# Level-1 sums of a two-level Strassen product made in PSUM instead of on VectorE

## The chip, the core and the metric

The kernel runs on one core of a Trainium2 chip. Its time is the device time of one execution in microseconds (us); less is better. The engines are TensorE (PE; its weight loads are shown as PEld), VectorE (DVE), ScalarE (ACT), GpSimd (POOL) and SyncE (SP). PE adds its products up in PSUM, eight banks of 128 partitions x 512 fp32 columns; DVE and ACT read and write PSUM and SBUF. DMAs are issued from SP and from ACT: an issue from ACT stands in ACT's queue among its other work.

## What is computed

Two graph layers over N = 3327 nodes with D = 512 features, in fp32, with a dense 3327 x 3327 matrix `adj`:

```python
# layer 0: attention with adj added twice to the scores
h = relu(layernorm(x));  q, k, v = h @ Wq.T + bq, h @ Wk.T + bk, h @ Wv.T + bv
x = x + softmax(q @ k.T / sqrt(D) + adj + adj, axis=-1) @ v
# layer 1: normalised convolution with A2 = adj + I
h = relu(layernorm(x));  temp = A2 @ h @ W.T
d = diagonal(A2) ** -0.5
x = x + relu((d[:, None] * A2 * d[None, :]) @ temp)
```

Up to about 620 us the kernel makes the scores and their exponentials. From there on it makes three large products of the same shape, called g = 0, 1, 2: the exponentials by h, A2 by h, and A2 by `temp` (scaled). The change lies in these three.

## The kernel before

**Two levels of Strassen (Winograd's form).** Each of the three products is split into 2 x 2 blocks and made from seven block products, in the order `ORDER` = p5, p1, p6, p7, p2, p3, p4 (level 1). Each of them is made for two strips s = 0, 1 of the output (quarter widths `Q` = 448 and 384 columns), again from seven products (level 2). The output stands transposed in SBUF as four regions per strip, r11, r12, r21, r22, in the buffers `cts`.

**Steps.** A (g, r, s) has seven steps: t = 0 to 5, which take the 26 row tiles in pairs, and t = None for the thirteenth row of tiles, without Strassen. A step t = 0 to 5 multiplies seven times (L918, L919; each product stands as two MATMUL records in the trace), into seven banks named p1 to p7 by level 2. At t=0 the order is p6, p7, p5, p2, p3, p4, p1, at t = 1 to 5 p1 is first. p1, p6, p7 and p5 end with t=5. The step t=None multiplies four times (L911), into p2, p3, p4 and p8, and p8 takes the bank that p1 had.

**Gathering.** At the end of t=5 `Gather.first` (L942) has ACT copy p1 to SBUF (L947) and DVE make three sums and differences with p6, p7, p5 (L948 to L951). At the end of t=None `rest` adds p2, p3, p4 and p8 to the four quarters (L964 to L967); L964 is the one that frees bank p2, L966 the one that frees p4. For p5 and p1 the result lands in a region at once (`place`). For the other five it lands in a spare buffer `to`, and `settle` (L969) does the level-1 sums on DVE, in instructions of 896 or 768 columns: for p6 r12 = to − r11 (L973), for p7 r21 = to + r12 (L975) and two more (L976, L977), for p2, p3 and p4 one addition to r11, r12 or r21 (L980). The very last product (g=2, p4, s=1) adds its banks straight into the region.

**The order of the work.** `run(k)` (L1230) writes out step k, and `in_order` (L1295) keeps each engine's instructions, ACT's and SP's too, in the order of the program. In a step: the DMA for the step three later; the loads named in `between` (those from ACT are L1018 in `attend_load` and L1088 in `finish_load`); the matmuls; the delayed stores `deliver` (L797, L93, from ACT); for t=None `rest`; then what is left for DVE: the sums of the left operands for the step two later (`four_sums`, L175 to L177, with L901 for the diagonal), `settle`, and the remaining tasks in `between` (right operands, L882 to L886 and L182 to L185; `Job`, L1002; `attend`, L1020; `attended`, L1028; `finish`, L1118).

**Work beside it.** In g = 0, from p3 strip 1 to the end, every step finishes one row of attention: `attend` multiplies by the value weights on PE (L1011) and normalises on DVE and POOL; one step later, t=None included, `attended` has DVE make `nb` (L206), ACT make the activation (L1030), and ACT issue its store (L1031). In g = 1, from p3 strip 1 to the start of g = 2, `Temp` multiplies by the weights of layer 1 (L1072, L1076, L1078). In g = 2 `finish` transposes and stores the rows of the result.

Of the kernel before, what the change touches and what calls it, by code (L numbers as in the profile page):

```python
# [29 lines left out]
ORDER = ("p5", "p1", "p6", "p7", "p2", "p3", "p4")  # L30
# [6 lines left out]
PAIRS = 6  # L37
# [3 lines left out]
Q = tuple(n * P // 2 for n in HT)  # L41
# [6 lines left out]
def graph_layers_kernel(  # L48
# [29 lines left out]
    nc = tc.nc  # L78
# [31 lines left out]
    def bank(k, name):  # L110
        return banks.tile([P, BW], F32, name=name, tag=f"bank{k}")
# [323 lines left out]
    ps = [bank(k, "mm") for k in range(DC)]  # L435
    begun = h_transposed(TURN[0], psum_ring(6, 7, 4, 5))
    weighed = half(12, [P, D], "weighed")
    for c in range(DC):
# [8 lines left out]
        for r in range(DC):  # L447
            nc.tensor.matmul(ps[r], w_q[c // 2][:, c % 2, r * P : (r + 1) * P], w_k[c // 2][:, c % 2],
                             start=c == 0, stop=c == DC - 1)
# [165 lines left out]
    steps = [(n, t) for n in range(len(groups)) for t in range(HALF)]  # L615
# [32 lines left out]
    with in_order(*(e.engine for e in (nc.vector, nc.tensor, nc.gpsimd, nc.sync))):  # L648
# [9 lines left out]
        k = len(steps)  # L658
# [28 lines left out]
    ROLE = {"p1": 0, "p6": 2, "p7": 4, "p5": 6, "p2": 7, "p3": 1, "p4": 5, "p8": 3}  # L687

    def seven():
        return {r: bank(ROLE[r], r) for r in ("p6", "p7", "p5", "p2", "p3", "p4", "p1")}  # L690
# [199 lines left out]
    class Step:  # L890


        def __init__(self, g, r, s, t, right):
            self.g, self.r, self.s, self.t, self.right = g, r, s, t, right

        def load(self):
            self.a, self.diagonals = left(self.g, self.s, A_OF[self.r], self.t)
# [9 lines left out]
        def multiply(self, ps):  # L907
            a, b, w = self.a, self.right.b, Q[self.s]
            if self.t is None:
                for k, (y, z) in enumerate(((0, 0), (0, 1), (1, 0), (1, 1))):  # L910
                    yield nc.tensor.matmul(ps[("p2", "p3", "p4", "p8")[k]][:, :w], b[:, z], a[:, 0, y],  # L911
                                           start=k == 3, stop=True)
                return
            o, first = self.o, [("p1", 0, a[:, 0, 0])]
            seven = [("p6", 5, o[:, 2]), ("p7", 6, o[:, 0]), ("p5", 4, o[:, 1]),
                     ("p2", 2, a[:, 1, 0]), ("p3", 3, o[:, 3]), ("p4", 7, a[:, 1, 1])]

            for r, i, m in seven + first if self.t == 0 else first + seven:  # L918
                yield nc.tensor.matmul(ps[r][:, :w], b[:, i], m, start=self.t == 0,  # L919
                                       stop=self.t == PAIRS - 1 and r in ("p1", "p5", "p6", "p7"))  # L920

    flags = []

    class Gather:


        def __init__(self, r, s, last):
            ct, hw, qw = cts[s], H[s], Q[s]

            def region(y, z):  # L930
                return [ct[y][2 * z + k] for k in range(2)]

            self.r, self.last, self.place = r, last, {"p5": (1, 1), "p1": (0, 0)}.get(r)
            self.to = region(*self.place) if self.place else [cts["to"][k][:, :hw] for k in range(2)]
            self.width = qw
            self.spots = ((0, slice(0, qw)), (1, slice(0, qw)), (0, slice(qw, hw)), (1, slice(qw, hw)))
            self.regions = [region(y, z) for y in range(2) for z in range(2)]

        def parts(self, of):

            return [of[k][:, w] for k, w in self.spots]

        def first(self, ps):

# [11 lines left out]
        def rest(self, ps, names=("p2", "p3", "p4", "p8")):  # L956
            p = {k: ps[k][:, : self.width] for k in ("p2", "p3", "p4", "p8")}
            if self.last:
                for o, k in zip(self.parts(self.regions[2]), p):
                    if k in names:  # L960
                        nc.vector.tensor_add(o, o, p[k])
                return
            c11, c12, c21, c22 = self.parts(self.to)
            nc.vector.tensor_add(c11, c11, p["p2"])  # L964
            nc.vector.tensor_sub(c12, p["p3"], c12)
            nc.vector.tensor_add(c21, c21, p["p4"])  # L966
            nc.vector.tensor_add(c22, c22, p["p8"])  # L967

        def settle(self):  # L969
            r11, r12, r21, r22 = self.regions  # L970
            for k, to in enumerate(self.to):
                if self.r == "p6":
                    yield nc.vector.tensor_sub(r12[k], to, r11[k])  # L973
                elif self.r == "p7":
                    yield nc.vector.tensor_add(r21[k], to, r12[k])  # L975
                    yield nc.vector.tensor_sub(r12[k], r22[k], r12[k])  # L976
                    yield nc.vector.tensor_sub(r22[k], r21[k], r22[k])  # L977
                elif not self.place and not self.last:
                    t = {"p2": r11, "p3": r12, "p4": r21}[self.r]
                    yield nc.vector.tensor_add(t[k], t[k], to)  # L980

    def where(i):

# [138 lines left out]
    every = (*range(PAIRS), None)  # L1122
    rights = {(g, r, t): Right(g, r, t) for g in range(3) for r in ORDER for t in every}
    steps = [Step(g, r, s, t, rights[g, r, t]) for g in range(3) for r in ORDER for s in range(2) for t in every]
# [3 lines left out]
    def number_of(g, r, s, t):  # L1128
        return ((g * len(ORDER) + r) * 2 + s) * len(every) + t
# [5 lines left out]
    for g in range(3):  # L1135
        for n, r in enumerate(ORDER):
            for t, e in enumerate(every):
                k = number_of(g, n, 0, t)
# [9 lines left out]
    for n, job in enumerate(jobs):  # L1148
        k = k0 + n * (k1 - k0) // len(jobs)
# [15 lines left out]
    k = number_of(0, 5, 1, 2)  # L1165
# [6 lines left out]
    k = number_of(1, 5, 1, 2)  # L1172
    for n in range(0, NT, 2):
        if steps[k].t is None:
            k += 1
        w = Temp(*ROW[n : n + 2])
# [5 lines left out]
    for (n, s, t), its in {  # L1182
# [4 lines left out]
        for i, when in zip(its, (between, within)):  # L1187
            if i is not None:
                k = number_of(2, n, s, t)
# [8 lines left out]
    k = number_of(1, 4, 0, 0)  # L1198
# [13 lines left out]
    banks_of, gathers = {}, {}  # L1212
    resting = []
# [6 lines left out]
    def first_of(parts):  # L1220
        while parts:
            for _ in parts[0]:
                yield
            parts.pop(0)

    def do(part, n=None):
        for _ in itertools.islice(part, n):
            pass

    def run(k):  # L1230
        step, now[0] = steps[k], k
        if k + 3 < len(steps):
            steps[k + 3].load()
        if step.t == 0:
            banks_of.update(seven())
        if not cts:
            set_up()
        if step.t is None:
            banks_of["p8"] = bank(ROLE["p1"], "p8")
        t = step.t  # L1240
        for what, args in between.get(k, ()):
            if "load" in what.__name__:
                what(*args)
        if t == PAIRS - 1:
            gathers[step.r, step.s] = Gather(step.r, step.s, k == len(steps) - 2)
        gatherer = gathers.get((step.r, step.s))
        weighs = any((k, j) in inserted for j in range(7))
        if k in sums_of and not waiting:
            do(sums_of.pop(k)())
        for j, _ in enumerate(itertools.chain((None,), step.multiply(banks_of))):  # L1250
            for w, n in inserted.get((k, j), ()):
                w.product(n)
            if j == 4 and t == PAIRS - 1 and gatherer.last:
                gatherer.first(banks_of)
            for what, args in within.get(k, ()) if j == 4 else ():
                what(*args)
            if j == 2 and k in sums_of:

                sums = sums_of.pop(k)()
                do(sums, 4)  # L1260
                waiting.insert(1, sums)
            elif weighs and j > 0:
                do(first_of(waiting), 2)
        deliver(k)
        if t is None:
            do(first_of(waiting))
            if gatherer.last:
                flags.append(nc.values_load(bad, min_val=0, max_val=1))
                for n, names in enumerate((("p2", "p3"), ("p4", "p8"))):
                    gatherer.rest(banks_of, names)  # L1270
                    for i in range(20 + 3 * n, 23 + 3 * n):
                        turn_last(i)
            else:
                gatherer.rest(banks_of)
        added = 2 + (t is None)
        waiting.append(steps[k + 2].sums() if k + 2 < len(steps) else iter(()))
        if t == PAIRS - 1 and not gatherer.last:
            do(first_of(waiting))
            gatherer.first(banks_of)
        if t is None and gatherer.r == "p7":  # L1280
            settle = gatherer.settle()
            resting.extend((itertools.islice(settle, 3), settle))
            added -= 1
        elif t is None:
            waiting.append(gatherer.settle())
        elif resting:
            waiting.append(resting.pop(0))
            added += 1
        waiting.append(flow([(what, args) for what, args in between.get(k, ()) if "load" not in what.__name__]))
        if (k + 1, 0) not in inserted and (k + 1, 1) not in inserted:  # L1290
            do(first_of(waiting))
        while len(waiting) > added:
            do(waiting.pop(0))
# [386 lines left out]
```

## Time and profile before

| | us |
|---|---|
| median of 3 runs (2164.09 to 2168.61) | 2165.39 |
| the profiled execution's own time | 2165.84 |
| its span, first to last instruction | 2164.1 |
| PE, matmuls | 2148.5 (99%) |
| DVE | 1675.6 (77%) |
| ACT | 237.0 (11%) |

The mean granted clock of PE is 0.999 of full speed. Matmuls of level 2 follow each other every 0.376 us (448 columns) or 0.323 us (384), two to a product. In the profile's lists a name such as L964 is a line of the kernel; "ACTq" is a DMA issue on ACT; a row of a timeline has start and length in us, engine, line, operation, output<-input, shapes, and in brackets the idle time of that engine before it and what ended it. Names like `part` and `ct` are buffers that share their place with others, and `p` stands for all banks p1 to p8.

### The profile page before, as it was taken

How to read it: one execution, taken by the hardware profiler on the slowest of the kernel's cores; microseconds unless marked ns; L12 is line 12 of the kernel's file. 1: busy time of each engine (PE TensorE's matmuls, PEld its weight loads, DVE VectorE, ACT ScalarE, POOL GpSimd, SP SyncE). 2: the span in 40 equal slices, each digit the busy share in tenths (PEclk: the TensorE clock that was granted, in tenths of full speed). 3: DMA queues.
4: the chain of work that ended last, by engine and by line, in shares of the span. 5: the costliest groups of instructions: out<-in, count | busy, mean ns of one | idle time of the engine just before them, and what ended most of it. 6: DMA issues, size and time to landing. Idle time of an engine off the chain costs nothing.

```text
span 2164.1 us, 20995 instructions
## 1 busy us (share of the span) xinstructions
PE 2148.5 (99%) x6364; PEld 1189.9 (55%) x6364; DVE 1675.6 (77%) x3270; ACT 237.0 (11%) x363; POOL 51.5 (2%) x62
## 2 busy tenths in 40 slices
PE   9999999999999999999999999999999999999998
PEld 5555555555555555555454555555666655555555
DVE  7479888888887688877778778886676667778686
ACT  5312211112110000000101000000011100000011
POOL 2000000000000000000111000000000000000000
PEclk9999999999999999999999999999999999999999
DMA  8678898888988899889797889886646468766695
GB/s 302 211 257 302 296 311 278 306 293 301 328 306 301 292 370 329 280 289 314 263 311 259 304 289 368 308 302 221 208 133 217 137 193 286 246 194 210 217 304 197
DMA packets 298670, 586.01 MB, mean 271 GB/s; under 512 B 31274, under 2 KB 166324, under 8 KB 298548
## 3 DMA queue, kind: packets, MB, share of 16 engines
q1 hardware_dynamic: 263254, 515.10, 70.8%
q10 hardware_dynamic: 35294, 69.48, 8.8%
q8 instruction: 53, 0.87, 0.2%
q14 instruction: 69, 0.57, 0.1%
HBM read 416.63 MB, written 167.84 MB: 270 GB/s over the span
## 4 chain that ended last, share of the span: by engine, by line
PE 93%; DVE 5%; DMA 1%; issue 1%; POOL 0%; SPq 0%; ACT 0%; DVEq 0%
PE p L919 55%; PE Y L553 13%; PE Z L553 6%; PE p L911 5%; PE p L1011 4%; PE pw L1072 3%; PE X L553 3%; PE Y L409 2%; PE Z L409 1%; PE pt L1101 1%; DVE part L175 0%; DMA rows<-row 0%; PE X L409 0%; DVE st L196 0%; DMA xt<-in_x_dram 0%
## 5 line engine op out<-in xcount | busy, mean ns | idle before, releaser
L919 PE MATMUL p<-part,b 128*128 128x448 f32 (+1 forms) x3528 | 1261.6, 513 | 0.4 <-DVE part L176 0.2
L919 PEld LDWEIGHTS p<-part,b 128*128 128x128 f32 x3528 | 668.0, 190 | 534.4 <-issue 283.5
L553 PE MATMUL Y<-qt,hp 128*128 128x448 f32 (+1 forms) x832 | 308.2, 513 | 2.1 <-DVE g L557 1.7
L175 DVE TENSOR_TENSOR part<-part 128x896 f32<-128x896 f32 (+1 forms) x252 | 256.8, 1019 | 57.0 <-DMA part<-p 24.6
L553 PEld LDWEIGHTS Y<-qt,hp 128*128 128x128 f32 x832 | 157.8, 190 | 135.9 <-issue 72.7
L553 PE MATMUL Z<-qt,hp 128*128 128x384 f32 (+1 forms) x416 | 162.3, 512 | 0.0
L177 DVE TENSOR_TENSOR part<-part,part 128x448 f32<-128x448 f32 (+1 forms) x219 | 129.4, 591 | 15.3 <-PE p L919 0.5
L176 DVE TENSOR_TENSOR part<-part,part 128x448 f32<-128x448 f32 (+1 forms) x219 | 129.4, 591 | 7.2
L911 PE MATMUL p<-part,b 128*128 128x448 f32 (+1 forms) x336 | 124.2, 513 | 0.0
L553 PEld LDWEIGHTS Z<-qt,hp 128*128 128x128 f32 x416 | 79.0, 190 | 66.2 <-issue 37.9
L557 DVE SCALAR_TENSOR_TENSOR g<-g,Y 128x384 f32<-128x384 f32 (+1 forms) x156 | 91.3, 585 | 29.9 <-PE Y L553 28.7
L911 PEld LDWEIGHTS p<-part,b 128*128 128x128 f32 x336 | 63.7, 190 | 53.5 <-issue 31.6
L947 ACT COPY part<-p 128x384 f32<-128x384 f32 (+1 forms) x33 | 16.6, 502 | 657.8 <-PE p L919 446.1
L553 PE MATMUL X<-qt,hp 128*128 128x384 f32 (+1 forms) x208 | 81.1, 512 | 0.0
L560 ACT ACTIVATE g<-g 128x768 f32<-128x768 f32 (+1 forms) x48 | 43.0, 896 | 347.1 <-DVE g L557 296.7
L1011 PE MATMUL p<-w,ct 128*128 128x512 f32 x136 | 61.8, 594 | 0.4 <-DVE part L1023 0.4
L948 DVE TENSOR_TENSOR part<-p,part 128x384 f32<-128x384 f32 (+1 forms) x33 | 19.3, 585 | 54.8 <-PE p L919 54.1
L553 PEld LDWEIGHTS X<-qt,hp 128*128 128x128 f32 x208 | 39.5, 190 | 33.1 <-issue 19.3
L1072 PE MATMUL pw<-w,rows 128*128 128x256 f32 x208 | 53.6, 380 | 0.8 <-DVE rows L1062 0.8
L1002 DVE TENSOR_TENSOR job<-job 128x896 f32<-128x896 f32 (+1 forms) x52 | 52.9, 1017 | 0.1
L202 POOL TENSOR_TENSOR rstd<-ve,mhalf 128x1 f32<-128x1 f32 x46 | 38.7, 844 | 555.8 <-DVE ve L200 520.2
L1072 PEld LDWEIGHTS pw<-w,rows 128*128 128x128 f32 x208 | 39.3, 190 | 20.6 <-issue 7.1
(199 smaller groups left out, 1684.7 us busy)
## 6 DMA issues: line engine op xcount, KB each, us to landing
part<-sum SPq DMA_DIRECT2D x104, 448.0 KB, 5.0
part<-p SPq DMA_DIRECT2D x91, 448.0 KB, 6.1
part<-sum SPq DMA_DIRECT2D x104, 384.0 KB, 3.8
part<-p SPq DMA_DIRECT2D x91, 384.0 KB, 4.0
part<-in_adjT_dram SPq DMA_DIRECT2D x78, 448.0 KB, 4.9
b<-row SPq DMA_DIRECT2D x234, 128.0 KB, 4.8
part<-in_adjT_dram SPq DMA_DIRECT2D x78, 384.0 KB, 3.8
g<-in_adjT_dram SPq DMA_DIRECT2D x52, 448.0 KB, 4.2
```

The costliest lines, as they stand in the source:

```text
L175: yield nc.vector.tensor_add(o[:, 0:2], g[:, 0:4:3], g[:, 1:2].to_broadcast([P, 2, g.shape[-1]]))
L176: yield nc.vector.tensor_add(o[:, 2], o[:, 1], g[:, 0])
L177: yield nc.vector.tensor_add(o[:, 3], o[:, 2], g[:, 2])
L409: nc.tensor.matmul(ps[:, :w], M[B[name]][:, c, o * P : (o + 1) * P], hp[k][:, A[name], c], start=start and c == 0, stop=c == 1, skip_group ...
L553: nc.tensor.matmul(ps[:, :wd], h_of(self.t, name, k), qt[B[name]][:, k], start=start and k == 0, stop=k == 1, skip_group_check=True)
L557: nc.vector.scalar_tensor_tensor(a[n], a[n], 2.0, ps[:, :wd], op0=ALU.mult, op1=ALU.add if sign > 0 else ALU.subtract)
L560: nc.scalar.activation(g[1], g[1], AF.Exp, **({"bias": pad} if self.t == HALF - 1 else {}))
L911: yield nc.tensor.matmul(ps[("p2", "p3", "p4", "p8")[k]][:, :w], b[:, z], a[:, 0, y], start=k == 3, stop=True)
L919: yield nc.tensor.matmul(ps[r][:, :w], b[:, i], m, start=self.t == 0, stop=self.t == PAIRS - 1 and r in ("p1", "p5", "p6", "p7"))
L1002: nc.vector.tensor_add(self.a, self.a, self.b)
L1011: nc.tensor.matmul(ps, cts[s][y][d][:, k * P : (k + 1) * P], w[d], start=d == 0, stop=d == DC - 1)
L1072: nc.tensor.matmul(ps, a, W[B[name]][:, c], start=new and c == 0, stop=c == 1, skip_group_check=True)
```

## The change

Before the level-2 products of one of the five late level-1 products begin, ACT writes a region's contents into banks p2, p3, p4 and, later, p8, multiplied by 1 or −1 (`SEEDED`), and the matmuls into these banks add to them from the first (`start` is off). `rest` then writes its four sums into the region where the result belongs (`INTO`), and of `settle` only the two other sums of p7 stay (L976, L977). p2, p3 and p4 are seeded at the top of step t=0, in `run` behind the loads of that step and ahead of its matmuls; p8 is seeded at t=5, behind `first`. In p1 strip 1 DVE clears p2, p3 and p4 over 448 columns with three memsets, at the same spot, and the matmuls add to that. The last product (g=2, p4, s=1) is left as it was.

```diff
+            self.seeded = r in SEEDED and (g, r, s) != (2, ORDER[-1], 1)
...
-                                           start=k == 3, stop=True)
+                                           start=k == 3 and not self.seeded, stop=True, skip_group_check=True)
...
+                seeded = r in ("p2", "p3", "p4") and (self.seeded or (self.r, self.s) == ("p1", 1))
+                yield nc.tensor.matmul(ps[r][:, :w], b[:, i], m, start=self.t == 0 and not seeded,
...
+    SEEDED = {"p6": (0, -1.0), "p7": (1, 1.0), "p2": (0, 1.0), "p3": (1, 1.0), "p4": (2, 1.0)}
+    INTO = {"p6": 1, "p7": 2, "p2": 0, "p3": 1, "p4": 2}
...
+        def seed(self, ps, names):
+
+            if self.r in SEEDED and not self.last:
+                j, sign = SEEDED[self.r]
+                for k, c in zip(("p2", "p3", "p4", "p8"), self.parts(self.regions[j])):
+                    if k in names:
+                        nc.scalar.mul(ps[k][:, : self.width], c, sign)
+            elif (self.r, self.s) == ("p1", 1):
+                for k in names:
+                    if k != "p8":
+                        nc.vector.memset(ps[k][:, : Q[0]], 0.0)
...
-            nc.vector.tensor_add(c11, c11, p["p2"])
-            nc.vector.tensor_sub(c12, p["p3"], c12)
-            nc.vector.tensor_add(c21, c21, p["p4"])
-            nc.vector.tensor_add(c22, c22, p["p8"])
+            o11, o12, o21, o22 = self.parts(self.regions[INTO[self.r]]) if self.r in INTO else (c11, c12, c21, c22)
+            nc.vector.tensor_add(o11, c11, p["p2"])
+            nc.vector.tensor_sub(o12, p["p3"], c12)
+            nc.vector.tensor_add(o21, c21, p["p4"])
+            nc.vector.tensor_add(o22, c22, p["p8"])
...
-            for k, to in enumerate(self.to):
-                if self.r == "p6":
-                    yield nc.vector.tensor_sub(r12[k], to, r11[k])
-                elif self.r == "p7":
-                    yield nc.vector.tensor_add(r21[k], to, r12[k])
+            if self.r == "p7":
+                for k in range(2):
                     yield nc.vector.tensor_sub(r12[k], r22[k], r12[k])
                     yield nc.vector.tensor_sub(r22[k], r21[k], r22[k])
-                elif not self.place and not self.last:
-                    t = {"p2": r11, "p3": r12, "p4": r21}[self.r]
-                    yield nc.vector.tensor_add(t[k], t[k], to)
...
-        if step.t is None:
-            banks_of["p8"] = bank(ROLE["p1"], "p8")
...
-        if t == PAIRS - 1:
-            gathers[step.r, step.s] = Gather(step.r, step.s, k == len(steps) - 2)
+        if t == 0:
+            gathers[step.r, step.s] = Gather(step.r, step.s, k == len(steps) - len(every))
+            gathers[step.r, step.s].seed(banks_of, ("p2", "p3", "p4"))
...
+        if t == PAIRS - 1:
+            banks_of["p8"] = bank(ROLE["p1"], "p8")
+            gatherer.seed(banks_of, ("p8",))
         if t is None and gatherer.r == "p7":
             settle = gatherer.settle()
-            resting.extend((itertools.islice(settle, 3), settle))
+            resting.extend((itertools.islice(settle, 2), settle))
```

More of the change, by code (lines that the diff above doesn't have):

```diff
@@ L918, in multiply @@
             for r, i, m in seven + first if self.t == 0 else first + seven:
-                yield nc.tensor.matmul(ps[r][:, :w], b[:, i], m, start=self.t == 0,
-                                       stop=self.t == PAIRS - 1 and r in ("p1", "p5", "p6", "p7"))
+                seeded = r in ("p2", "p3", "p4") and (self.seeded or (self.r, self.s) == ("p1", 1))
+                yield nc.tensor.matmul(ps[r][:, :w], b[:, i], m, start=self.t == 0 and not seeded,
+                                       stop=self.t == PAIRS - 1 and r in ("p1", "p5", "p6", "p7"), skip_group_check=True)
     flags = []
+    SEEDED = {"p6": (0, -1.0), "p7": (1, 1.0), "p2": (0, 1.0), "p3": (1, 1.0), "p4": (2, 1.0)}
+    INTO = {"p6": 1, "p7": 2, "p2": 0, "p3": 1, "p4": 2}
     class Gather:
@@ L934, in __init__ @@
             self.to = region(*self.place) if self.place else [cts["to"][k][:, :hw] for k in range(2)]
-            self.width = qw
+            self.width, self.s = qw, s
             self.spots = ((0, slice(0, qw)), (1, slice(0, qw)), (0, slice(qw, hw)), (1, slice(qw, hw)))
```

## The prediction, as put on record before the result

> **What bounds the kernel now.** I read the engine totals first, then busy time by stretch, then the timeline of each engine around the places that the change touches. The totals:
>
> ```profile
> PE 2148.5 (99%) x6364; PEld 1189.9 (55%) x6364; DVE 1675.6 (77%) x3270; ACT 237.0 (11%) x363; POOL 51.5 (2%) x62
> ```
>
> TensorE (PE) is busy 99% of a span of 2164.1 us. The part that the change touches runs from 619 us on; busy time by stretch (length, then busy us and instructions of PE, weight load, VectorE, ScalarE, GpSimd):
>
> ```profile
> 619.00:1134.00 515.00, 513.77 (x1443) 272.74 (x1442) 405.72 (x760) 22.13 (x37) 21.23 (x17) 1.00 0.88 302
> 1134.00:1520.00 386.00, 386.00 (x1082) 205.30 (x1081) 308.86 (x569) 15.16 (x23) 10.81 (x10) 1.00 0.85 291
> 1520.00:1760.00 240.00, 238.99 (x827) 156.13 (x826) 155.21 (x369) 26.66 (x57) 0.00 (x0) 1.00 0.56 179
> ```
>
> From 619 to 1760 us PE is idle 1.23 + 0.00 + 1.01 = 2.24 us. After that its idle time is almost all the end, behind the last matmul (2155.95 us). VectorE (DVE) is busy about 80% here, but it seldom holds PE up. So a shorter DVE can give back some 2 us, and the end of the kernel is moved by whatever makes PE wait. The question is what the new waits of PE cost.
>
> **What goes.** The level-1 sums of `settle`: in the table of groups by shape L973 has 12 instructions with 6.3 + 5.5 us, L975 12 with 6.5 + 5.7, L980 34 with 18.8 + 9.1 + 5.5. Together 58 instructions and 57.4 us of DVE. They lie beside PE's work; on the path they are worth at most the 2.24 us above. I take 1.0 us (PE's waits that follow a late DVE, such as L1011 on L1023 near 1037 us), bounds 0 and 2.24.
>
> **What comes.** ScalarE (ACT) writes four quarter regions into banks for each of the 29 seeded products (five products, two strips, three graphs, less the last): 116 instructions. The nearest rows are ACT's copies from SBUF to SBUF, L597: 0.565 us for 448 columns, 0.508 for 384 (from PSUM, L947: 0.531 and 0.478; L771, the same `mul` on 512 columns, 0.630). That is some 62 us on an engine with 237 us of work; the sum does not matter, the places do. The matmul count stays the same, and `start` changes nothing in what PE streams.
>
> The fourth bank (p8) is seeded at t=5, right behind ACT's copy L947. From the end of that copy to PE's first p8 matmul the trace of before has at least 2.18 us, and 4 to 8 us at most places; 0.57 us fits. I cost it at nothing.
>
> The other three banks are seeded at the top of step t=0. Before: DVE's L964 frees bank p2, then PE may write it, behind p6, p7 and p5 of t=0. Now ACT stands between: L964, hand-over (0.04 us, as L964 starts behind PE's p2 where DVE is idle), 0.5 us of ACT, hand-over (taken as 0.05). Some 0.65 us (448) or 0.60 (384) must fit between the end of L964 and PE's first p2 matmul. Where DVE keeps up that gap is 3.4 us, so nothing is lost. I measured it at all 29 places. Tight ones: graph 0, p6 strip 0 (0.64 us) and strip 1 (0.48): together 0.02 + 0.12 = **0.14 us**, bounds 0 and 0.3. Graph 2, p4 strip 0 (0.29) and graph 0, p4 strip 0 (0.75) fall under the next point.
>
> **What is queued ahead on ACT.** The order on ACT is that of the program, and the seeds stand in `run` behind (a) what step t=None put on ACT, (b) the loads issued from ACT at t=0. In graph 0 one `attended` (L1030, then its store L1031) falls on t=None of p3 strip 1 and of p4 strip 0, and L1030 waits for `nb` (L206), which DVE makes after the next step's sums. Today nothing of PE waits for it. The first place, DVE and then ACT:
>
> ```profile
> 1027.23 0.62 DVE L177 TENSOR_TENSOR part<-part,part 128x448 f32<-128x448 f32 x1
> 1027.78 1.82 DVE L980 TENSOR_TENSOR part<-part,part 128x768 f32<-128x768 f32 x2
> 1029.51 0.68 DVE L886 TENSOR_TENSOR b<-b,rows 128x512 f32<-128x512 f32 x1
> ...
> 1031.17 0.15 DVE L206 SCALAR_TENSOR_TENSOR nb<-mv,rstd 128x1 f32<-128x1 f32 x1
> ```
>
> ```profile
> 1031.35 0.81 ACT L1030 ACTIVATE h<-xt,nb,rstd 128x512 f32<-128x512 f32 x1 [9.35 <-DVE nb L206]
> 1032.20 0.33 ACTq L1031 DMA_DIRECT2D row<-h  x1
> 1032.57 0.44 ACTq L1018 DMA_DIRECT2D part<-in_x_dram  x1
> ```
>
> ```profile
> 1022.64 5.42 PE L919 MATMUL p<-part,b 128*128 128x448 f32 x14
> ```
>
> PE begins t=0 at 1022.64 and reaches p2 at 1024.89. ACT is through with L1030, L1031 and the load L1018 at 1033.01. L980 goes: 1029.51 − 1027.78 = 1.73 us earlier. Then the seed: 1033.05 + 0.565 + 0.05 − 1.73 = 1031.93. PE waits 1031.93 − 1024.89 = **7.0 us**. At the second place (p4 strip 1) L1018 ends at 1087.27; L980 (1082.42 to 1084.43) goes, 2.01 us; 1087.31 + 0.508 + 0.05 − 2.01 = 1085.86 against p2 at 1080.46: **5.4 us**.
>
> The third place is p4 strip 0 of graph 2, with two loads for `finish` at t=0:
>
> ```profile
> 2085.07 0.34 ACTq L93 DMA_DIRECT2D out_dram<-r  x1
> 2085.50 1.90 ACTq L1088 DMA_DIRECT2D xr<-x1d  x2
> ```
>
> Seeds from 2087.44, p2 ready at 2088.05, PE there at 2085.80: **2.25 us**. If the second load did not wait, 0.9; so 0.9 to 2.8. Elsewhere ACT's queue is free: at p2 strip 1 of graph 2 (L1118 ends at 1987.9, p2 at 1989.14), and in the weights stage of graph 1 the seeds come before the first `Temp` product, whose L1076 then ends near 1565, still ahead of the L1078 that needs it (1565.80).
>
> **The memsets.** In p1 strip 1 of each graph DVE clears three banks, in the program behind the sums that close t=None. The first instruction of the next step's sums marks the spot; in graph 2:
>
> ```profile
> 1793.57 0.62 DVE L967 TENSOR_TENSOR ct<-ct,p 128x448 f32<-128x448 f32 x1
> ...
> 1796.36 0.28 DVE L901 TENSOR_TENSOR part<-part,ident 128x128 f32<-128x128 f32 x1
> ```
>
> `rest` ends with L967, the sums of the step after next follow, and with 1796.36 the next step's work begins. The memset would start there, and PE reaches p2 at 1795.30. No memset of PSUM is in the trace. Rows: 128 columns of SBUF 165 ns, 26 columns 80 ns, so 0.83 ns a column: 0.43 us for 448; below it the 165 ns, above it 0.62 us of a sum of that width. With 0.43 and 0.05: 1.06 + 0.48 = 1.54 us. Graph 1 (1265.47 against 1264.41) gives 1.54, graph 0 (724.31 against 723.45) 1.34. Together **4.4 us**, bounds 3.6 and 5.1.
>
> **The clock.** The granted clock stays full up to the end and falls to half at 2160.8 us, 4.8 us after the last matmul ended. At the start 16 matmuls of 128 columns take 3.57 us, 0.22 us apart where later ones are 0.11 apart; full pace comes at 7.0 us, so 5.8 us of work ran at half pace and lost 2.9 us. A wait of 7.0 us is longer than 4.8, and one of 5.4 just. I take 2.9 us for the first and half of that for the second: **4.4 us**, bounds 0 and 6.8.
>
> The Trainium skill ("TensorE: Matmul & The Clock Gate", Part 1, "What's actually happening") puts the fall after one idle window of some 3.4 us and the return after a busy one of the same length, free-running: as an estimate from that page both waits would halve the clock and lose 1.7 to 3.4 us each, 3.4 to 6.8 in place of my 4.4. The tail's 4.8 us lies within one to two such windows. Its page "ScalarE: Activation LUTs" (rules for kernel authors) speaks against the change in another way: it gives adds and multiplications to VectorE; no run here shows DVE writing the seeds.
>
> **Sum.** 7.0 + 5.4 + 2.25 + 4.4 + 0.14 + 4.4 − 1.0 = 22.6 us. The profiled execution took 2165.84 us (1.7 us lie around its span), so 2188.4; the median of the runs shown is 0.45 us lower: **2188**.
>
> **Rivals.**
> - *A, as above*, 0.70. Lowest: 6.9 + 5.3 + 0.9 + 3.6 + 0 + 0 − 2.2 = 14.5, so 2180; highest 7.1 + 5.5 + 2.8 + 5.1 + 0.3 + 6.8 = 27.6, and 2193 (the first two terms with 0.1 us either way for the hand-overs).
> - *B, the seeds are not held up behind `attended`* (its `nb` comes sooner than I read, or the seeds overtake it), 0.12: 2.25 + 4.4 + 0.14 − 1.0 = 5.8 us, 2171. For it: ACT is idle 89% of the span. Against: ACT's rows stand in program order in the trace.
> - *C, not slower: the seeds and memsets are all in time*, and DVE's missing 57.4 us only take away its lateness. It decides if the seed reaches p2 within the gaps above (0.3 to 3.4 us) everywhere. Price: at most −2.24 us, 2163, within 0.2% of before; 0.05, of which 0.02 goes to a gain over 0.2% by something that I don't see. That the change moves nothing at all gives the same time.
> - *D, more waits than I found*: every one of the 29 places loses some 0.3 us (a wait of PE just met or just missed), 8 to 9 us on top: 2197; 0.13.
>
> The range 2172 to 2197 takes in A and its bounds, most of B and half of D. A difference of 0.2% (4.3 us) is about what a measurement can tell from no change: faster 0.02, same 0.03, slower 0.95.
>
> **What would show it.** In the profile after: ACT some 60 us busier and DVE some 54 less; PE idle at p4 strips 0 and 1 of graph 0 behind ACT's seeds, 5 to 7 us each, with L1030 just ahead of the seeds; about 1.5 us behind a memset near 724, 1275 and 1810 us; a granted clock under 1 for some us after the long waits. If PE shows no such waits the order on ACT was read wrongly (B or C); if the waits are there but the clock stays full, some 4 us less.

## The result: 1.1% slower

The median of five runs is 2189.18 us (2185.73 to 2193.57), against 2166.01 us for the kernel before on the same chip: a ratio of 1.0107, 95% interval 1.0095 to 1.0118. The forecast was 2188 (22.6 us more than before; measured were 23.2). The profiled execution took 2186.82 us, with a span of 2185.0.

The totals of the changed kernel (engine, busy us, share of the span, instructions; DVE is 49 us shorter, ACT 58 us longer, PE has the same number of instructions):

```profile
PE 2153.1 (99%) x6364; PEld 1191.6 (55%) x6364; DVE 1626.3 (74%) x3221; ACT 295.2 (14%) x479; POOL 52.9 (2%) x62
```

Busy time by stretch, with the borders moved by what was lost so far (columns as in the rows of before):

```profile
619.00:1150.00 531.00, 516.83 (x1441) 274.03 (x1440) 390.77 (x746) 41.98 (x76) 21.25 (x17) 0.99 0.84 293
1150.00:1538.00 388.00, 386.44 (x1083) 205.41 (x1082) 297.59 (x558) 30.92 (x54) 10.81 (x10) 1.00 0.84 289
1538.00:1780.00 242.00, 240.02 (x829) 156.61 (x828) 148.90 (x362) 31.00 (x66) 0.00 (x0) 1.00 0.56 179
```

PE's idle time in them (length less PE's busy time) is 14.17 + 1.56 + 1.98 = 17.7 us, where it was 2.24; most of it lies in graph 0, and there alone the clock is under 1.

PE's waits in the same profile (who waited for whom: us in total, times, longest):

```profile
PE p L921 <- DVE part L177: 6.9, 1, 6.9
PE p L921 <- ACT p L954: 6.4, 2, 5.2
PE p L921 <- DVE p L958: 4.5, 3, 1.6
...
PE pw L1084 <- ACT ts L1088: 1.4, 1, 1.4
```

L921 is the seven products' matmul, L954 the seed, L958 the memset, L1084 a matmul of `Temp` and L1088 the ScalarE product that reads it (L1072 and L1076 before). None of these rows is in the profile of before. The first row names L177, a sum on DVE. The timeline shows that this is the wrong one of several releasers: L177 ended at 1027.06 us, and PE went on at 1031.13. DVE, ACT and PE around the first place (p4 strip 0 of graph 0), with the columns of the timelines shown for before:

```profile
1026.44 0.62 DVE L177 TENSOR_TENSOR part<-part,part 128x448 f32<-128x448 f32 x1
1026.99 0.68 DVE L886 TENSOR_TENSOR b<-b,rows 128x512 f32<-128x512 f32 x1
...
1028.64 0.15 DVE L206 SCALAR_TENSOR_TENSOR nb<-mv,rstd 128x1 f32<-128x1 f32 x1
```

```profile
1028.83 0.81 ACT L1042 ACTIVATE h<-xt,nb,rstd 128x512 f32<-128x512 f32 x1 [7.61 <-DVE nb L206]
1029.67 0.33 ACTq L1043 DMA_DIRECT2D row<-h  x1
1030.04 0.44 ACTq L1030 DMA_DIRECT2D part<-in_x_dram  x1
1030.53 0.55 ACT L954 ACTIVATE p<-ct 128x448 f32<-128x448 f32 x1 [0.89 <-ACT h L1042]
```

```profile
1021.84 2.42 PE L921 MATMUL p<-part,b 128*128 128x448 f32 x6
1031.13 5.32 PE L921 MATMUL p<-part,b 128*128 128x448 f32 x8 [6.88 <-DVE part L177]
```

The settle (L980 before) is gone between L177 and L886, so `nb` comes 1.7 us sooner, counted from PE's start of t=0. ACT then runs `attended` (now L1042 and L1043), the load (now L1030) and only then the seed, which ends at 1031.08. PE made the six records of p6, p7 and p5 and stood still until 1031.13. At p4 strip 1 it is the same: PE is idle for 5.24 us until L954 is done. The third place, ACT (L1100 is the load for `finish`):

```profile
2104.92 0.98 ACTq L1100 DMA_DIRECT2D xr<-x1d  x2
2105.95 0.55 ACT L954 ACTIVATE p<-ct 128x448 f32<-128x448 f32 x1 [4.64 <-DMA b<-row]
```

The two loads took 0.98 us here, where before they took 1.90: the second waited less. And p1 strip 1 of graph 2, DVE and then PE:

```profile
1813.53 0.56 DVE L177 TENSOR_TENSOR part<-part,part 128x384 f32<-128x384 f32 x1
1814.17 1.38 DVE L958 MEMSET p<- 128x448 f32 x3
```

```profile
1814.66 4.78 PE L921 MATMUL p<-part,b 128*128 128x384 f32 x14 [1.56 <-DVE p L958]
```

**An account by the spacing of the matmuls.** PE's idle time leaves out what is lost in the pipeline and at a low clock. So I took, for each matmul of both traces, the time from its start to the next start, less the usual spacing of that width (0.376 us for 448 columns; for 384 it is 0.3225, the mean of 0.322 and 0.323, which alternate). Below, "by the spacing" means this excess. Summed from 700 us on, this excess is 4.4 us before and 27.0 us after: 22.6 us more. Ahead of 700 us, where nothing was changed, it was 1.7 us less in this execution (a wait of 1.57 us near 513 us in the profile of before is missing here); so the spans differ by 20.9 us.

| term | forecast, us | by the spacing, us |
|---|---|---|
| p4 strip 0, graph 0 | 7.0 | 7.04 |
| p4 strip 1, graph 0 | 5.4 | 5.40 |
| p4 strip 0, graph 2 | 2.25 | 1.29 |
| three memsets | 4.4 | 1.52 + 1.72 + 1.72 = 4.96 |
| tight places (p6, graph 0) | 0.14 | none seen |
| clock behind the two long waits | 4.4 | 2.15 + 1.67 = 3.8 |
| second `Temp` product, graph 1 | 0 | 1.54 |
| old waits that went | −1.0 | about −1.9 |

### The profile page after: what moved, and what is told of

Same layout as the page of the kernel before. It is cut to its first block, busy times and chain, and to the rows that moved or that the text cites. A ratio compares the mean times of both kernels' runs of the same rounds, so it can differ in the third digit from the quotient of the medians.

```text
span 2185.0 us, 21072 instructions
## 1 busy us (share of the span) xinstructions
PE 2153.1 (99%) x6364; PEld 1191.6 (55%) x6364; DVE 1626.3 (74%) x3221; ACT 295.2 (14%) x479; POOL 52.9 (2%) x62
## 4 chain that ended last, share of the span: by engine, by line
PE 93%; DVE 4%; DMA 1%; issue 1%; ACT 0%; POOL 0%; ACTq 0%; SPq 0%; DVEq 0%
PE p L921 55%; PE Y L553 13%; PE Z L553 6%; PE p L912 5%; PE p L1023 4%; PE pw L1084 3%; PE X L553 3%; PE Y L409 2%; PE Z L409 1%; DVE part L175 1%; PE X L409 1%; PE pt L1113 1%; DMA wk<-in_wk_dram 0%; DMA rows<-row 0%; DVE part L176 0%
## 5 line engine op out<-in xcount | busy, mean ns | idle before, releaser
L921 PE MATMUL p<-part,b 128*128 128x448 f32 (+1 forms) x3528 | 1266.5, 514 | 17.9 <-DVE part L177 6.9
L921 PEld LDWEIGHTS p<-part,b 128*128 128x128 f32 x3528 | 669.3, 191 | 555.5 <-issue 293.2
L175 DVE TENSOR_TENSOR part<-part 128x896 f32<-128x896 f32 (+1 forms) x252 | 257.0, 1020 | 72.9 <-DMA part<-sum 30.0
L177 DVE TENSOR_TENSOR part<-part,part 128x448 f32<-128x448 f32 (+1 forms) x219 | 129.5, 591 | 14.9
L912 PE MATMUL p<-part,b 128*128 128x448 f32 (+1 forms) x336 | 124.2, 513 | 0.0
L912 PEld LDWEIGHTS p<-part,b 128*128 128x128 f32 x336 | 63.7, 190 | 53.5 <-issue 31.8
L964 ACT COPY part<-p 128x384 f32<-128x384 f32 (+1 forms) x33 | 16.6, 502 | 528.6 <-PE p L921 461.3
L1035 DVE SCALAR_TENSOR_TENSOR part<-p,rs,part 128x512 f32<-128x512 f32 x20 | 15.0, 750 | 59.0 <-PE p L1023 59.0
L954 ACT ACTIVATE p<-ct 128x448 f32<-128x448 f32 (+1 forms) x84 | 43.0, 528 | 94.9 <-DVE ct L982 48.0
L1084 PE MATMUL pw<-w,rows 128*128 128x256 f32 x208 | 53.5, 380 | 0.4 <-DVE rows L1074 0.4
```

The lines of the kernel that those rows point to most:

```text
L175: yield nc.vector.tensor_add(o[:, 0:2], g[:, 0:4:3], g[:, 1:2].to_broadcast([P, 2, g.shape[-1]]))
L177: yield nc.vector.tensor_add(o[:, 3], o[:, 2], g[:, 2])
L954: nc.scalar.mul(ps[k][:, : self.width], c, sign)
L1084: nc.tensor.matmul(ps, a, W[B[name]][:, c], start=new and c == 0, stop=c == 1, skip_group_check=True)
```

## Experiments

The theory on trial, A: the seeds stand behind `attended` and loads in ACT's queue, and the memsets behind the sums in DVE's; PE waits for the queue. Rival R1: what costs is the hop itself, another engine between DVE and PE at each seeded bank. R2: DVE's sums hold PE up at the first place, as the row of waits says. R3: a shorter DVE is worth more than PE's idle time shows. Ratios are to the kernel before, run beside on the same chip.

**e1, ACT's seeds right behind `rest`.**

```diff
...
             else:
                 gatherer.rest(banks_of)
+                banks_of.update(seven())
+                then = steps[k + 1]
+                gathers[then.r, then.s] = Gather(then.r, then.s, k + 1 == len(steps) - len(every))
+                if then.r != "p1":
+                    gathers[then.r, then.s].seed(banks_of, ("p2", "p3", "p4"))
...
```

> Only ACT's seeds are moved: they stand right behind rest of the product before, ahead of attended and of the loads; the memsets stay where the change put them. Theory A (the seeds wait in ACT's queue behind attended and loads): the waits of 7.0, 5.4 and 1.3 us at p4 go (0.4 stays at the third place), and with them the fall of the clock, 3.8 us: 2189.2 - 17 = 2172 us, ACT's seeds done within 0.7 us of L982. Rival R1 (the extra engine between DVE and PE costs something at every seeded place, wherever the seeds stand): 2187 to 2190. Rival R2 (PE waits at the first place for DVE's sums L177, as the profile's releaser says): 6.9 us and its clock stay, about 2182.

Measured: 2172.33 us, ratio 1.0028 (1.0017 to 1.0038). Nothing was taken away from ACT or DVE; the same seeds stand elsewhere, and 17 us are gone (by the spacing 27.0 falls to 10.0 us). R1 falls for ACT's seeds, and R2 with it: the row with L177 is gone, though the same sums are still made at the same place.

**e2, the memsets right behind `rest`**, ACT's seeds left where the change had them (the edit of e1 with `then.r == "p1"`).

> Only the three memsets of p1 strip 1 are moved, right behind rest, ahead of the sums; ACT's seeds stay. Theory A: the three waits on the memset, 5.0 us by the spacing of the matmuls, go: 2184 us. Rival R1 (clearing or seeding a bank costs PE something in itself): 2188 to 2189.

Measured: 2187.59 us, ratio 1.0098 (1.0083 to 1.0114), too near to the change to tell, where 2184 was expected. In its profile the waits on L958 are gone, but the third place took 2.85 us instead of 1.29, with 1.53 us of slow clock behind it, and the clock behind the two long waits cost 4.6 us instead of 3.8:

```profile
2104.67 2.08 ACTq L1100 DMA_DIRECT2D xr<-x1d  x2
2106.79 0.55 ACT L954 ACTIVATE p<-ct 128x448 f32<-128x448 f32 x1 [6.20 <-DMA b<-row]
```

The price of that place hangs on how long ACT spends on the two loads: 0.98 us in the profile of the change, 2.08 here. So the next runs take it out of the comparison.

**e3, both moves.**

> Both moves. Theory A: the two gains add up, 2189.2 - 22 = 2167 us, with 1.4 us left at the first Temp product of graph 1 and some 0.5 us at p4 and p6, so within 0.2% of before. Rival R1: 2186 or more. A gain over before of more than 0.2% would need DVE's lateness to cost more than the 2.2 us of PE idle time that the profile of before shows.

Measured: 2166.53 us, ratio 1.0003 (0.9994 to 1.0012). The whole loss is gone within the interval. At the first place, ACT and PE:

```profile
1025.71 1.48 ACT L954 ACTIVATE p<-ct 128x448 f32<-128x448 f32 x3 [2.17 <-DMA row<-h]
```

```profile
1024.16 5.42 PE L921 MATMUL p<-part,b 128*128 128x448 f32 x14
```

The three seeds run beside p6, p7 and p5, and the fourteen records of t=0 are one unbroken piece, as in the kernel before. The excess from 700 us on is 4.6 us, against 4.4 before and 27.0 with the change.

**e4, the kernel before without its level-1 sums.** `settle` keeps L976 and L977 alone, and `rest` writes into the region, so the result lacks the level-1 sums.

> The kernel before without its 58 level-1 sums on DVE, and with nothing in their place: rest writes into the region and the earlier content is lost, so this leaves out part of the computation. It prices DVE's relief alone. Theory A: 1.0 us less than before (0 to 2.2), 2165 us. Rival R3 (a shorter DVE is worth more than PE's idle time shows): 2161 or less.

Measured: 2165.00 us, ratio 0.9998 (0.9989 to 1.0007). DVE's busy time is 1622.7 us instead of 1675.6, and nothing comes of it that a measurement can tell (by the spacing 4.4 falls to 2.9 us). R3 falls: with nothing in place of the sums the gain is at most 0.11%, 2.4 us, by the interval, and the change could hardly have won more.

**e5, the seeds ahead of the loads of t=0**, still behind `attended`: in `run` the block with `seed` moves above the loop over the loads.

> The change, with the seeds ahead of the loads that ACT issues at t=0 instead of behind them; attended stays ahead. Theory A: the two long waits lose one load each, 7.04 to 6.6 and 5.40 to 5.0 us; the third (graph 2, p4) falls to 0.4 us and no longer depends on when a load's turn comes; the rest stays. 2165.0 + 6.6 + 5.0 + 0.4 + 5.0 (memsets) + 1.5 (Temp) + 0.4 + 3.4 (clock) = 2187 us. Rival R1 (the hop costs, not the queue): as the change, 2189. This is also the base of the next three.

Measured: 2187.29 us, ratio 1.0101 (1.0085 to 1.0116). By the spacing the waits are 6.54 and 4.91 us, each shorter by the load that now stands behind (0.50 and 0.49), and the third is 0.35. The time alone doesn't tell e5 from the change; the shorter waits in its profile do.

**e6, e5 with the memsets right behind `rest`.**

> e5 with the three memsets right behind rest. It settles the price of the memsets, which e2 left open because its third place took 2.85 us and a fall of the clock. Theory A: 5.0 us less than e5, 2182. If the memsets cost nothing on the path (R1): as e5.

Measured: 2182.41 us, ratio 1.0077 (1.0063 to 1.0090); 4.9 us less than e5, and the three waits on the memset are gone from its profile. The two intervals just overlap, but waits and time agree: this settles what e2 left open. Whether the three banks have to be cleared at all, no run shows.

**e7, PE kept busy in the two long waits.**

```diff
...
+            idle = (self.g, self.r, self.t) == (0, "p4", 0) and bank(ROLE["p8"], "idle")
             for r, i, m in seven + first if self.t == 0 else first + seven:
+                if idle and r == "p2":
+                    for n in range(8 - self.s):
+                        nc.tensor.matmul(idle[:, :w], b[:, 4], o[:, 1], start=True, stop=True)
...
```

> e5 with idle matmuls (8 and 7, into a free bank, read by nobody) between p5 and p2 of t=0 at the two long waits: 6.0 of 6.6 and 4.5 of 5.0 us are filled. They take no time from the path if the wait ends when the seeds are there. Theory A (a wait of that length costs the clock, too): full clock after both, 3 to 4 us less than e5, 2183.5. If the slow stretch behind the waits has another cause (seeds that still arrive one by one): as e5.

Measured: 2185.42 us, ratio 1.0079 (1.0065 to 1.0093). Busy time of PE in stretches around the two waits (length, PE busy, granted clock, DMA share, GB/s), first the change, then e7:

```profile
1022.00:1031.13 9.13, 2.26 (x7) 0.85 0.80 251
1031.13:1036.00 4.87, 4.87 (x8) 0.57 0.97 359
...
1093.50:1098.00 4.50, 4.46 (x9) 0.64 0.68 236
```

```profile
1022.00:1036.00 14.00, 13.63 (x38) 1.00 0.81 246
1086.00:1098.00 12.00, 11.77 (x36) 1.00 0.68 234
```

In the change the clock falls during the wait and stays at half in the matmuls behind it. In e7 PE reaches p2 as late as in e5, 8.80 us behind the start of t=0 in both at the first place, but the clock never falls there. So the slow matmuls are the clock's doing, and not seeds that come one by one. In the profiles e5 lost 5.5 us behind the two waits and e7 none to speak of: between the same two matmuls near 1015 and 1200 us e7's execution is 5.3 us shorter than e5's. Its whole time shows nothing of it, because it lost 4.4 us more ahead of 700 us, where the two kernels are the same. The medians show 1.9 us, with intervals that overlap. What is shown is the mechanism; the size is between 2 and 5 us.

**e8, e5 with as much DVE work as before**: `settle` adds into the spare buffer, which nobody reads, where the level-1 sums used to stand.

> e5 with DVE additions of the size and at the places of the old level-1 sums, into the spare buffer, where nobody reads them. Theory A (nb stands behind DVE's sums, so each us of DVE ahead of it lengthens the wait): 1.7 and 2.0 us more at the two long waits, 0 to 1.7 us of clock, 0.5 us of lost relief: 2191 to 2193. If the seeds wait for nothing that DVE's load moves (R1): 2187 to 2188.

Measured: 2190.73 us, ratio 1.0116 (1.0100 to 1.0131); by the spacing the two waits are 8.28 and 6.92 us, 1.74 and 2.01 more than in e5. DVE at the first place, and the seed:

```profile
1027.44 0.62 DVE L177 TENSOR_TENSOR part<-part,part 128x448 f32<-128x448 f32 x1
1027.98 1.82 DVE L992 TENSOR_TENSOR part<-part,part 128x768 f32<-128x768 f32 x2
1029.72 0.68 DVE L886 TENSOR_TENSOR b<-b,rows 128x512 f32<-128x512 f32 x1
```

```profile
1032.77 0.55 ACT L954 ACTIVATE p<-ct 128x448 f32<-128x448 f32 x1 [0.40 <-ACT h L1045]
```

L992 stands where L980 stood, and the wait grows by just its length (L980 held `nb` up by 1.73 us before). The chain DVE, `nb`, `attended`, seed, PE is closed by this.

**e9, e3 and the `Temp` wait.** Where a `Temp` product opens a step t=0, the seeds go behind its ScalarE product:

```diff
...
             for w, n in inserted.get((k, j), ()):
                 w.product(n)
+                if (t, j, n) == (0, 0, 0):
+                    gatherer.seed(banks_of, ("p2", "p3", "p4"))
...
```

> e3 (seeds and memsets right behind rest), and where a product of Temp opens a step t=0 the seeds stand behind its first ScalarE product instead of ahead of it. Theory A: the 1.5 us wait of the second Temp product in graph 1 goes, 2166.5 - 1.5 = 2165 us, within 0.2% of before, since DVE's relief is worth 1 us at most (e4). Rival R3 (DVE's relief shows once no seed is late): 2161 or less.

Measured: 2165.68 us, ratio 1.0006 (0.9997 to 1.0015). The wait of 1.54 us is gone from the profile (3.4 us of excess are left from 700 us on), but the time is that of before within the interval. No version here beats the kernel before: PE's work is the same, and only 4.4 us of excess from 700 us on were there to be had.

**e10, e3 with the seeds on DVE**: `nc.vector.tensor_scalar` with a multiplication in place of `nc.scalar.mul`.

> e3 with the seeds written by DVE instead of ScalarE, at the same places. DVE then has rest, three seeds of some 0.45 us behind one another, and its 57 us back. By the gaps of the profile of before (0.29 to 1.6 us between the end of L964 and PE's p2; the seed of p2 comes 2.0 to 2.15 us behind it) PE waits at seven places, 8.0 us in all, and the Temp wait of 1.5 us and e3's 0.9 us go: 2166.5 + 8.0 - 2.4 = 2172 us. If the engine that seeds does not matter once the seeds are early: 2166.

Measured: 2175.10 us, ratio 1.0048 (1.0035 to 1.0062), 10 us over before where 6 were expected. A seed on DVE, and PE's waits:

```profile
L954 DVE TENSOR_SCALAR p<-ct x84: 551/619/625, 750.4 to 2125.0; 128x448 f32<-128x448 f32 x60, 128x384 f32<-128x384 f32 x24
```

```profile
PE p L921 <- DVE p L954: 3.9, 4, 1.5
PE p L912 <- DVE p L954: 2.4, 5, 0.9
...
PE pw L1084 <- DVE rows L1074: 1.3, 1, 1.3
```

A seed of 448 columns takes 0.62 us and not 0.45, and the seed of p8, which I had left out, makes L912 wait, too. The `Temp` wait did not go, as expected, but changed its cause: its matmul now waits for operands (L1074) that DVE makes behind the three seeds. By the spacing the excess from 700 us on is 12.4 us, 8.0 more than before; this profile is of the fastest execution (2172.52 us), and what the others lost on top it can't show. For the seeds ACT is the better engine than DVE; where they stood in ACT's queue was the mistake.

## Why the prediction was right, point by point

- **What bounds the kernel**: right. DVE's relief was taken as 1.0 us with 2.24 as its bound; e4 shows 0.9 us by the medians (an interval that takes in zero), 1.5 by the spacing. DVE's busy time fell by 52.9 us in e4, not 57.4; nothing hung on that.
- **The fourth bank (p8)**: right, it cost nothing; no wait of L912 for a seed is in the profile.
- **What is queued ahead on ACT**: right in mechanism (e1, e5, e8) and in size, 7.04 and 5.40 us. The sum was made from rows of before, less the L980 that goes; e8 put L980's time back and the waits grew by it.
- **The third place**: right in mechanism, too large here (2.25 against 1.29). The length of the second load was taken from one execution; e2 had 2.85. The bounds given were 0.9 to 2.8: 1.29 lies within them, 2.85 just above.
- **The memsets**: right, 4.4 against 4.96. A memset took 0.432 us, as taken (0.43). What was short is its start: I put it where the next sum had begun, 0.48 us behind the start of L177, and it begins 0.64 us behind it (1814.17 against 1813.53).
- **Tight places**: the 0.14 us at p6 was not seen. In the profile of the change DVE's read of p2 (L982, L964 before) ended 2.58 and 2.16 us ahead of PE's p2 there, not 0.64 and 0.48. The gap depends on a load: ahead of p6 strip 0 DVE waited for it (L175, `DMA part<-p`) 6.04 us in the profile of before and 2.45 in that of the change, and 4.73 in e3's, where the gap is 1.89. One profile was too little to cost this term. At p2 strip 1 of graph 2, costed at nothing, the seed was done only 0.05 us ahead of PE.
- **The clock**: right that it falls in both waits (the granted clock under e7), 3.8 us (2.15 + 1.67) against 4.4 (2.9 + 1.5). The closeness is partly luck: the same two places lost 4.6, 5.5, 4.4 and 4.1 us in the profiles of e2, e5, e6 and e8, and the shorter waits of e5 lost the most. The bound that a wait must near 4.8 us was wrong: see the last section. The prediction's estimate from the Trainium skill's page on the clock gate, 3.4 to 6.8 us, takes in the measured 3.8, and the 5.5 of e5, too.
- **"In the weights stage ... L1076 then ends near 1565, still ahead of the L1078 that needs it"**: wrong. ACT, then PE, in the change:

```profile
1579.86 1.48 ACT L954 ACTIVATE p<-ct 128x448 f32<-128x448 f32 x3 [4.28 <-DMA row<-ts]
1581.28 0.45 ACT L1088 ACTIVATE ts<-pw,sd 128x256 f32<-128x256 f32 x1
```

```profile
1578.74 1.67 PE L921 MATMUL p<-part,b 128*128 128x448 f32 x4
1581.79 1.13 PE L1084 MATMUL pw<-w,ct 128*128 128x256 f32 x4 [1.38 <-ACT ts L1088]
```

  I looked at the reader of the result on DVE (L1078) and not at the bank. The second product goes into the other half of the same bank and waits until ACT has read the first half. Three seeds ahead of that read are 1.48 us, and 1.54 us are lost; e9 takes them back.

- **The rivals**: B and C fall, since PE does wait behind ACT's queue at the places that A named (e1, e5, e8). D falls, too: of the 29 seeded products PE waited behind the first seeds at three, those of A. The stated range begins at 2172, so B's own price, 2171, lies just outside it, and not "most of B" inside.

The mechanism was right; that the sum met to 0.1 us is luck. The forecast of 22.6 us met the 22.6 us of the spacing because the missed `Temp` wait (+1.5) and the memsets (+0.6) were made up for by the third place (−1.0), the old waits that went (−0.9) and the clock (−0.6); some 0.5 us of small change behind the shorter waits is in the 22.6, too.

## What to carry to other kernels

An engine with 11% of work is no free place: what counts is what stands ahead of the new instruction in that engine's order, and for whom that waits. Look for in-order neighbours that nothing waited for until now; a new wait behind them inherits their whole chain, here DVE, `nb`, an activation and two DMA issues. When work is put on a side engine for PE's sake, write it out right behind what frees its operand, unless something that PE needs sooner stands there (the `Temp` read, e9).

## What the runs showed of the hardware that I had not expected

**How short a wait halves the clock.** The tail of before let me expect a fall only near 4.8 us of idle PE. From 500 us on, a single wait between dense matmuls (by the spacing) did this in the profiles: at 1.14 to 2.12 us (memsets, `Temp`, the stage boundary near 620 us in three runs) the clock stayed full; waits of 2.61, 2.75, 2.85, 2.89 and 3.17 us, at that boundary and at the third place of e2, were each followed by 1.5 to 3.1 us of lost time at half the clock. These are single executions; nothing between 2.12 and 2.61 us was seen. Behind all these waits and the long ones the clock stood at half for 3.41, 6.83 or 10.24 us in the traces. The Trainium skill ("TensorE: Matmul & The Clock Gate", "Part 1: The HAM clock gate") asks for an idle window of some 3.4 us; these runs show a fall at waits shorter than that.

**A multiplication into PSUM.** For 448 columns ScalarE's seed takes 0.542 us, DVE's `tensor_scalar` 0.621 (mean of 60 each), DVE's memset 0.432. The skill's rule for kernel authors ("ScalarE: Activation LUTs"), which gives multiplications to VectorE and argues from bf16, is not borne out for this fp32 case: DVE was slower on the same operands, and its queue was the fuller one (e10).
